# Attention followed by a mixture-of-experts layer: Q and K in fp16 parts, a new order of the softmax steps in the loop, and a new way to the scale factors in the lead-in

## The chip, the core and the metric

The kernel runs on one NeuronCore of one Trainium2 chip. The metric is device time in microseconds (us) of one launch. The engines are TensorE (PE in the profile, with PEld for its weight loads), VectorE (DVE), ScalarE (ACT), GpSimd (POOL) and SyncE (SP, which here only issues DMAs). Each has a queue of its own and works on it by itself; they meet through semaphores.

## The reference, cut to what matters

One sequence of S = 2048 rows and 256 columns goes through two residual blocks. The change touches the first:

```python
q = layernorm(x) @ dequant(wq) + bq          # 16 heads of 128; k and v likewise
scores = einsum('bqhd,bkhd->bhqk', q, k) / sqrt(128)
attn = softmax(scores, axis=-1)
out = einsum('bhqk,bkhd->bqhd', attn, v)     # 16 heads side by side: 2048 columns
y = out @ dequant(wo) + bo
x = x + layernorm(y)
```

`dequant(w)` is a matrix of 4-bit codes times a scale per 32 rows and column. The second block (`x + layernorm(ffn(layernorm(x)))`) routes each row to two of eight experts of width 176. Everything is float32 in the reference.

## The kernel before, in words

To keep accuracy with fast matmuls, each float32 operand is written as a high and a low part in a narrower type, and a product is made as three matmuls: high by high, high by low, low by high.

**Lead-in** (lines 221 to 374). The four chunks of x (512 rows each) are loaded, normalized (`ln0_stats`, `ln0_norm`), transposed by PE (`ln0_tr`) and split in fp16 parts `xnT` (`ln0_high` on ACT, `ln0_low` on DVE). The scales of the first pair of heads are spread over the partitions by a small matmul (`scale_bcast`), copied by ACT (`scale_s`) and multiplied with the codes on POOL (`dequant`). A power of two `sig`, taken from the largest scale of V, is found by an all-reduce over the partitions on POOL (line 341) and a few DVE steps; it keeps V's fp16 parts in range. Biases of Q and K are loaded by SP with one element per partition and head (lines 243 and 244).

**Projections.** `proj_qk` (line 179) makes 512 columns of K or Q for a head: four matmuls into one PSUM bank, ACT writes the high part with the bias (line 193, type fp32r), DVE the low part (line 194). `proj_v` (line 199) does the same for V in fp16 without a bias (lines 216 and 217). DVE's part is put into `pending` and issued by the next `flush()`.

**Attention loop** (lines 611 to 665). It runs over NS = 256 tiles g = 16 h + t: head h, and 128 query rows t. For a tile:

- `scores_half` twice: six matmuls per 1024 keys (lines 388, 389, 392; three PSUM buffers), then DVE's row maximum (line 393); `negmax` (line 399).
- `softmax`: ACT's exponentials of both halves, with row sums (line 406), into `p`.
- `recip`: DVE adds the two sums and inverts (lines 413 and 416).
- `high_part`: ACT writes p times the inverse as fp16 `ph` (line 420), SP transposes it by DMA into `pt`.
- `low_part`: the rest p/sum - ph as fp16 `pl`, 1536 columns on DVE (line 432), 512 on POOL (lines 438 and 439), and SP transposes that.
- `pv_part`: the product with V for a block of four tiles, 16 key chunks at three matmuls (lines 455 to 457); it is cut into eight `pv_unit`s per block, two units per pass, and runs PVLAG = 13 units behind. At the end of a block ACT and DVE write the output's parts (lines 463 and 464), and POOL issues their store.
- `fill`: one piece of projection for the next head or block (table `QK` for K and Q; V in between).

The order is written by hand (`manual_schedule`), so each engine's queue holds the instructions in the order of the code. One pass g of the loop before issues: s0(g) and its maximum; recip(g-1); pending parts; a PV unit; **high(g-1)**; s1(g) and its maximum; negmax(g); **exp(g)**; a PV unit; **low(g-1)**; fill(g).

**Tail.** It runs from line 943 on: the output projection reads the attention output back from DRAM (`load_oi`), then layernorm, router and experts. Its tiles `at` (line 681) and one `oi` tile (line 605) use the buffers of Q's tiles.

Of the kernel before, what the change touches and what calls it, by code (L numbers as in the profile page):

```python
# [20 lines left out]
S = 2048  # L21
# [16 lines left out]
def sandwich(  # L38
# [24 lines left out]
    # ---------------------------------------------------------------- constants  # L63
# [7 lines left out]
    bqT = const.tile([128, NH], F32)  # L71
    bkT = const.tile([128, NH], F32)
    sig = const.tile([128, 4], F32)
# [10 lines left out]
    ident_h = const.tile([128, 128], HP)  # L84
    iota8 = const.tile([128, 8], F32)
    one3 = const.tile([3, 128], F32)
    bvT = const.tile([128, NH], F32)
# [6 lines left out]
    def tail_consts(i):  # L94
        if i == 0:
            nc.sync.dma_start(out=bvT, in_=bv.rearrange("(h p) -> p h", p=128))
# [4 lines left out]
            nc.gpsimd.memset(one3, 1.0)  # L101
        else:
            nc.gpsimd.tensor_copy(ident_h, ident)
# [37 lines left out]

    def scale_s(which):
        f = sig[:, 1:2] if which == "v" else 1.0 / XS
        ps, sc, cd = raw[(0, which)]
        nc.scalar.activation(sc, ps, AF.Copy, scale=f)
        raw[(0, which)] = (sc, cd)

    def dequant(p, which):
        sc, cd = raw.pop((p, which))
        f = sig[:, 1:2] if which == "v" else 1.0 / XS  # L150
# [11 lines left out]
    # ------------------------------------------- LN of x, transposed in H and L  # L162
    # ------------------------------------------------------------- projections
# [15 lines left out]
    def proj_qk(which, h, b, tag="pj"):  # L179
        w = W[(h // 2, which)]  # L180
        bias = (bqT if which == "q" else bkT)[:, h : h + 1]
        ps = proj_psum(tag)
        col = bass.ts(h % 2, 128)
        n = 0
        for kc in range(2):
            for hl in range(2):
                nc.tensor.matmul(  # L187
                    ps, w[:, kc, col], xnT[:, 4 * b : 4 * b + 4, hl * 2 + kc, :],
                    start=(n == 0), stop=(n == 3),
                )  # L190
                n += 1
        t = kqv.tile([128, 2, 512], F32R, name=which + "T", bufs=8 if which == "k" else 2)
        nc.scalar.activation(t[:, 0, :], ps, AF.Identity, bias=bias)
        pending.append(lambda: nc.vector.scalar_tensor_tensor(
            t[:, 1, :], ps, bias, t[:, 0, :].bitcast(F32), ALU.add, ALU.subtract
        ))
        (Q if which == "q" else K)[(h, b)] = t
# [23 lines left out]
    with tc.tile_pool(name="start", bufs=4) as st:  # L221
# [3 lines left out]
        smax = st.tile([128, 128], F32, bufs=1)  # L225
        sc8 = st.tile([8, 3, 256], F32, bufs=1)
        nc.scalar.dma_start(out=s8, in_=sel8)
        for c in range(4):
            nc.sync.dma_start(out=xts[c], in_=xv[:, c])
        cds = {}  # L230
        for i, (which, codes, scales) in enumerate(
# [8 lines left out]
        nc.scalar.dma_start(  # L240
            out=smax, in_=wv_scales.rearrange("b (c n) -> (b c) n", n=128)
        )
        nc.sync.dma_start(out=bkT, in_=bk.rearrange("(h p) -> p h", p=128))
        nc.sync.dma_start(out=bqT, in_=bq.rearrange("(h p) -> p h", p=128))

        make_identity(nc, ident)
        def scale_bcast(which):
            i, cd = cds[which]
            if which == "v":
                ps = psA.tile([128, 512], F32, name="scv", tag="pv")  # L250
            else:
                ps = psS.tile([128, 2, 512], F32, name="scb", tag="s", bufs=3)[:, 0]
# [7 lines left out]
        sm = st.tile([128, 4], F32, bufs=1)  # L260
# [57 lines left out]
        def ln0_low(c):  # L318
# [5 lines left out]
        scale_bcast("k")  # L324
        scale_bcast("q")
        ln0_stats(0)
        ln0_stats(1)
        scale_s("k")
        scale_s("q")
        ln0_norm(0, nc.vector)  # L330
        ln0_tr(0)
        ln0_nb(1)
        ln0_norm(1, nc.scalar)
        ln0_tr(1)
        scale_bcast("v")
        dequant(0, "k")
        nc.vector.tensor_reduce(sm[:, 0:1], smax, AX.X, ALU.max)
        ln0_stats(2)
        ln0_high(0)
        nc.vector.tensor_scalar(sm[:, 1:2], sm[:, 0:1], 1e-30, None, ALU.max)  # L340
        nc.gpsimd.partition_all_reduce(
            sm[:, 2:3], sm[:, 1:2], 128, bass_isa.ReduceOp.max
        )
        ln0_stats(3, lambda: ln0_nb(2))
        dequant(0, "q")
        nc.vector.tensor_scalar(
            sm.bitcast(I32)[:, 3:4], sm.bitcast(I32)[:, 2:3], 0x7F800000, None,
            ALU.bitwise_and,
        )
        ln0_norm(2, nc.scalar)  # L350
        nc.vector.tensor_scalar(sig[:, 2:3], sm[:, 3:4], 0.125, None, ALU.mult)
        ln0_low(0)
        ln0_high(1)
        ln0_tr(2)
        nc.vector.reciprocal(sig[:, 0:1], sig[:, 2:3])
        ln0_norm(3, nc.vector)
        nc.vector.tensor_scalar(sig[:, 1:2], sig[:, 0:1], 1.0 / XS, None, ALU.mult)
        ln0_low(1)
        ln0_high(2)
        scale_s("v")  # L360
        ln0_low(2)
        proj_qk("k", 0, 0)
        ln0_tr(3)
        flush()
# [9 lines left out]
        dequant(0, "v")  # L374
# [4 lines left out]
    # --------------------------------------------------------------- attention  # L379
# [18 lines left out]
    def negmax(m):  # L398
        nc.vector.tensor_scalar(  # L399
            m[:, 2:3], m[:, 0:1], m[:, 1:2], -ISQ, ALU.max, ALU.mult  # L400
        )

    def softmax(h, t, ss, m):
        p = soft.tile([128, S], F32, name="p")
        for half in range(2):
            nc.scalar.activation(  # L406
                p[:, bass.ts(half, 1024)], ss[half].rearrange("p a b -> p (a b)"),
                AF.Exp, bias=m[:, 2:3], scale=ISQ, accum_out=m[:, 3 + half : 4 + half],
# [19 lines left out]
    def low_part(h, t, m, p, ph):  # L428
        pieces = 2 if h == 0 and t < 6 else 1
        cv = S - pieces * POOL_COLS  # L430
        pl = soft.tile([128, S], HP, name="pl")
        nc.vector.scalar_tensor_tensor(  # L432
            pl[:, :cv], p[:, :cv], m[:, 6:7], ph[:, :cv], ALU.mult, ALU.subtract
        )
        for c in range(cv, S, POOL_COLS):
            cs = slice(c, c + POOL_COLS)
            pr = soft.tile([128, POOL_COLS], F32, name="pr", bufs=1)
            nc.gpsimd.tensor_scalar(pr, p[:, cs], m[:, 6:7], 1.0, ALU.mult, ALU.mult)  # L438
            nc.gpsimd.tensor_tensor(pl[:, cs], pr, ph[:, cs], ALU.subtract)  # L439
# [32 lines left out]
    def fill(h, t):  # L472
# [22 lines left out]
    # ------------------------------- what the tail needs, made during the last head  # L495
# [75 lines left out]
    # ------------------------------------------------------------- attention loop  # L571
    PVLAG = 13
# [8 lines left out]
    def late(t):  # L581
# [22 lines left out]
        if t == 15:  # L604
            load_oi(0, 1, 1, "qT")
# [5 lines left out]
    for g in range(NS + 2):  # L611
# [20 lines left out]
        if prev is not None:  # L632
            hl = high_part(*prev)
# [44 lines left out]
    def op_mm(b, half, js, tag="pj"):  # L678
        if js[0] == 0:
            if half == 0:  # L680
                AT[b] = kqv.tile([128, 4, D], F32, name="at", tag="qT", bufs=2)
# [14 lines left out]
        if js[-1] == 3:  # L696
# [3 lines left out]
                at[:, tt], ps, sig[:, 2:3],  # L700
# [245 lines left out]
    nc.scalar.activation(sig[:, 3:4], sig[:, 2:3], AF.Sigmoid)  # L946
# [159 lines left out]
```

## Time and profile before

| what | value |
|---|---|
| runs | 1885.74, 1888.68, 1892.19 us; median 1888.68 |
| profiled execution | span 1897.5 us from first to last instruction; no other time of it is recorded |
| instructions | 25913 |
| granted PE clock, mean | 0.994 |
| PE, DVE, ACT, POOL busy | 1832.9, 1640.9, 1328.2, 883.7 us |
| first score matmul | 36.2 us |
| row maxima (line 393), first and last | 38.0 and 1600.1 us |
| exponentials (line 406) | 512 of 1.11 us, each followed by 0.19 us for the row sum |
| high part (line 420) | 256 of 2.00 us |
| low part on DVE (line 432), 1536 columns | 250 of 2.27 us in the mean, the shortest 1.82 |
| low part on POOL (line 438, line 439) | 262 of 0.72 and 262 of 1.86 us |
| DMA queues | 81.9% of 16 engines' span on the hardware queue that carries most transfers |

Where a row of the profile names an operation, it shows the output and the inputs by the program's names (`ph<-p,m`), the shape and type of each, how often, and the mean duration. PE's matmuls are pipelined, so their durations overlap; how far apart their starts lie says more. An idle time "<-" names what ended it; "issue" there means that the profile shows nothing waited for. Durations of neighbouring rows on DVE and ACT overlap by about 0.1 us too.

### The profile page before, as it was taken

To read this page: it belongs to the slowest core of one execution; us is meant where nothing else is said; L and a number is where in the kernel's file an instruction comes from. 1 tells how busy PE (TensorE), PEld (TensorE's weight loads), DVE (VectorE), ACT (ScalarE), POOL (GpSimd) and SP (SyncE) were. 2 spreads that over 40 slices of the span, in tenths; PEclk is the share of its full clock that TensorE was granted. 3 is DMA by queue.
4 is the path that set the end of the run, shared out by engine and by line. 5 is a ranking of instruction groups with operands and counts; after the bars stand their busy time and mean duration, and the time that the engine had idled before them with its cause. 6 is when DMAs were issued, how large, how long until landed. Compare 5 with 4: busy or idle time off the path is not lost.

```text
span 1897.5 us, 25913 instructions
## 1 busy us (share of the span) xinstructions
PE 1832.9 (97%) x8886; PEld 1161.5 (61%) x8886; DVE 1640.9 (86%) x2293; ACT 1328.2 (70%) x1730; POOL 883.7 (47%) x732
## 2 busy tenths in 40 slices
PE   5899999999999999999999999999999999899998
PEld 3555556555565565655655556655556555588887
DVE  5999998999999999999999999999999987468566
ACT  4877788778787778787878788777878777123232
POOL 2853465445444554455445544554444565233222
PEclk8999999999999999999999999999999999999999
DMA  2999999999999998899989988999899999982121
GB/s 75 192 188 179 179 207 184 188 184 194 192 184 182 208 202 186 183 193 204 183 174 199 205 180 187 190 210 185 181 186 192 222 222 243 257 250 70 51 68 56
DMA packets 1147220, 342.20 MB, mean 180 GB/s; under 512 B 1077008, under 2 KB 1137328, under 8 KB 1147088
## 3 DMA queue, kind: packets, MB, share of 16 engines
q1 hardware_dynamic: 1139152, 321.57, 81.9%
q0 software_dynamic: 5216, 16.81, 3.7%
q10 hardware_dynamic: 2720, 2.17, 0.4%
q8 instruction: 70, 1.15, 0.3%
q14 instruction: 62, 0.51, 0.1%
HBM read 53.08 MB, written 18.94 MB: 38 GB/s over the span
## 4 chain that ended last, share of the span: by engine, by line
PE 48%; DVE 9%; ACT 4%; DMA 4%; issue 3%; SPq 1%; POOL 0%; ACTq 0%; DVEq 0%; POOLq 0%
PE s L389 6%; PE s L388 6%; PE s L392 6%; PE pv L455 6%; PE pv L456 6%; PE pv L457 6%; PE gup L845 5%; DVE pl L432 4%; DMA pt<-pl 3%; PE pj L187 3%; ACT ph L420 3%; DVE m L393 2%; PE dps L884 2%; PE pj L206 1%; PE op L690 1%
## 5 line engine op out<-in xcount | busy, mean ns | idle before, releaser
L420 ACT ACTIVATE ph<-p,m 128x2048 f16<-128x2048 f32 x256 | 512.6, 2003 | 240.3 <-issue 134.9
L393 DVE TENSOR_REDUCE m<-s 128x1 f32<-128x1024 f32 x512 | 623.2, 1217 | 60.9 <-PE s L392 58.1
L406 ACT ACTIVATE p<-s,m 128x1024 f32<-128x1024 f32 x512 | 565.3, 1110 | 80.6 <-DVE m L399 76.4
L432 DVE SCALAR_TENSOR_TENSOR pl<-p,m,ph 128x1536 f16<-128x1536 f32 (+1 forms) x256 | 575.8, 2249 | 47.1 <-ACT ph L420 21.1
L439 POOL TENSOR_TENSOR pl<-pr,ph 128x512 f16<-128x512 f32 x262 | 486.5, 1857 | 264.7 <-issue 142.2
L388 PE MATMUL s<-kT,qT 128*128 128x512 f32 x1024 | 485.1, 474 | 5.3 <-ACT p L406 5.3
L389 PE MATMUL s<-kT,qT 128*128 128x512 f32 x1024 | 403.8, 394 | 0.0
L455 PE MATMUL pv<-pt,v 128*128 128x512 f16 x1024 | 393.4, 384 | 2.2 <-DVE o L464 2.0
L456 PE MATMUL pv<-pt,v 128*128 128x512 f16 x1024 | 388.7, 380 | 2.9 <-DMA pt<-pl 1.7
L457 PE MATMUL pv<-pt,v 128*128 128x512 f16 x1024 | 388.6, 379 | 0.0
L438 POOL TENSOR_SCALAR pr<-p,m 128x512 f32<-128x512 f32 x262 | 187.3, 715 | 329.5 <-DVE m L416 307.1
L392 PE MATMUL s<-kT,qT 128*128 128x512 f32 x1024 | 317.2, 391 | 0.0
L388 PEld LDWEIGHTS s<-kT,qT 128*128 128x128 f32 x1024 | 193.3, 189 | 79.0 <-ACT p L406 10.1
L392 PEld LDWEIGHTS s<-kT,qT 128*128 128x128 f32 x1024 | 192.2, 188 | 45.1
L389 PEld LDWEIGHTS s<-kT,qT 128*128 128x128 f32 x1024 | 193.5, 189 | 33.3
L455 PEld LDWEIGHTS <-v 128*128 128x128 f16 x1024 | 99.4, 97 | 185.7 <-issue 116.5
L457 PEld LDWEIGHTS <-v 128*128 128x128 f16 x1024 | 100.3, 98 | 121.2 <-issue 1.5
L456 PEld LDWEIGHTS <-v 128*128 128x128 f16 x1024 | 101.2, 99 | 75.3 <-issue 4.7
L859 POOL TENSOR_TENSOR hh<-sg,hh 128x512 fp32r<-128x512 f32 x42 | 54.5, 1299 | 143.6 <-ACT hh L858 106.6
L467 POOL DMA_DIRECT2D ot_d<-o x63 | 37.2, 590 | 172.8 <-DVE o L464 172.7
L858 ACT CAST hh<-sg 128x512 fp32r<-128x512 f32 (+1 forms) x45 | 27.5, 611 | 116.0 <-DVE sg L870 115.9
L406 ACT ACTIVATION_READ_ACCUMULATOR p<-s,m 128x1 f32 x512 | 99.7, 195 | 0.0
(160 smaller groups left out, 1727.5 us busy)
## 6 DMA issues: line engine op xcount, KB each, us to landing
oi<-ot_d SPq DMA_DIRECT2D x32, 512.0 KB, 5.9
ot_d<-o POOLq DMA_DIRECT2D x63, 256.0 KB, 5.4
pt<-ph SPq DMA_TRANSPOSE x256, 4.1
pt<-pl SPq DMA_TRANSPOSE x256, 4.0
cu<-ct_d SPq DMA_DIRECT2D x16, 256.0 KB, 3.7
xt<-in_L_attn_x SPq DMA_DIRECT2D x4, 512.0 KB, 5.2
wos<-in_L_attn_wo_scales ACTq DMA_DIRECT2D x32, 64.0 KB, 4.2
woc<-in_L_attn_wo_codes SPq DMA_DIRECT2D x8, 256.0 KB, 3.4
```

Source lines behind the costliest of these rows:

```text
L388: nc.tensor.matmul(s[:, j, :], q[:, 0, qc], k[:, 0, :], start=True, stop=False)
L389: nc.tensor.matmul(s[:, j, :], q[:, 0, qc], k[:, 1, :], start=False, stop=False)
L392: nc.tensor.matmul(s[:, j, :], q[:, 1, qc], k[:, 0, :], start=False, stop=True)
L393: nc.vector.tensor_reduce(m[:, half : half + 1], s.rearrange("p a b -> p (a b)"), AX.X, ALU.max)
L406: nc.scalar.activation(p[:, bass.ts(half, 1024)], ss[half].rearrange("p a b -> p (a b)"), AF.Exp, bias=m[:, 2:3], scale=ISQ, accum_out=m[: ...
L420: nc.scalar.activation(ph, p, AF.Copy, scale=m[:, 6:7])
L432: nc.vector.scalar_tensor_tensor(pl[:, :cv], p[:, :cv], m[:, 6:7], ph[:, :cv], ALU.mult, ALU.subtract)
L438: nc.gpsimd.tensor_scalar(pr, p[:, cs], m[:, 6:7], 1.0, ALU.mult, ALU.mult)
L439: nc.gpsimd.tensor_tensor(pl[:, cs], pr, ph[:, cs], ALU.subtract)
L455: nc.tensor.matmul(ps, vh, d[:, :, c, :], start=(c == 0), stop=False)
L456: nc.tensor.matmul(ps, vh, d[:, :, 16 + c, :], start=False, stop=False)
L457: nc.tensor.matmul(ps, vl, d[:, :, c, :], start=False, stop=(c == 15))
```

## The change

It does five things.

1. Q and K tiles become fp16 (`HP`) in place of fp32r. Their weights and biases are divided by powers of two `sig[:, 0]`, one each for Q, K and V, and the scale of the exponential and of `negmax` becomes a tensor `ssc`. In the loop (`wide=soft`) ACT writes the float32 projection to a scratch tile `t32`, and POOL makes both parts from it; in the lead-in ACT and DVE make them as before.
2. `low_part` is one DVE instruction over all 2048 columns; POOL's share and its scratch go. The addition of the two row sums goes from DVE to POOL (`row_sum`).
3. The order of a pass of the loop: s0(g); pending parts; PV unit; s1(g); negmax(g); exp(g); PV unit; **fill(g); recip(g-1); high(g-1); low(g-1); row_sum(g)**. `PVLAG` is 15, the loop has one more pass; `p` has three buffers, `ph` two.
4. The lead-in finds the three powers of two with PE: a maximum over scales and biases per partition on DVE, a transpose, a maximum and a bit mask on three partitions, and a matmul with a row of ones that spreads them. The scales of K and Q, not only V's, now wait for it. The biases come in as 48 rows and are transposed by PE.
5. In the tail `at` and one `oi` tile move to other buffers.

```diff
@@ proj_qk
-        t = kqv.tile([128, 2, 512], F32R, name=which + "T", bufs=8 if which == "k" else 2)
-        nc.scalar.activation(t[:, 0, :], ps, AF.Identity, bias=bias)
-        pending.append(lambda: nc.vector.scalar_tensor_tensor(
-            t[:, 1, :], ps, bias, t[:, 0, :].bitcast(F32), ALU.add, ALU.subtract
-        ))
+        t = kqv.tile([128, 2, 512], HP, name=which + "T", bufs=8 if which == "k" else 2)
+        if wide is None:
+            nc.scalar.activation(t[:, 0, :], ps, AF.Identity, bias=bias)
+            pending.append(lambda: nc.vector.scalar_tensor_tensor(
+                t[:, 1, :], ps, bias, t[:, 0, :], ALU.add, ALU.subtract
+            ))
+        else:
+            t32 = wide.tile([128, 512], F32, name="t32", bufs=1)
+            nc.scalar.activation(t32, ps, AF.Identity, bias=bias)
+            nc.gpsimd.tensor_copy(t[:, 0, :], t32)
+            nc.gpsimd.tensor_tensor(t[:, 1, :], t32, t[:, 0, :], ALU.subtract)
...
+        for i, scales in enumerate((wq_scales, wk_scales, wv_scales)):
+            nc.scalar.dma_start(
+                out=smax[:, i], in_=scales.rearrange("b (c n) -> (b c) n", n=128)
+            )
+        for i, bias in enumerate((bq, bk, bv)):
+            nc.scalar.dma_start(
+                out=b48[16 * i : 16 * i + 16], in_=bias.rearrange("(h p) -> h p", p=128)
+            )
...
-        nc.scalar.dma_start(
-            out=smax, in_=wv_scales.rearrange("b (c n) -> (b c) n", n=128)
-        )
-        nc.sync.dma_start(out=bkT, in_=bk.rearrange("(h p) -> p h", p=128))
-        nc.sync.dma_start(out=bqT, in_=bq.rearrange("(h p) -> p h", p=128))
...
+        def sig_bias():
+            ps = psA.tile([128, 512], F32, name="bps", tag="pj")
+            nc.tensor.transpose(ps[:, :48], b48, ident[:48, :48])
+            sgp["b"] = ps
+
+        def sig_local():
+            ps = sgp["b"][:, :48].rearrange("p (i h) -> p i h", i=3)
+            nc.vector.tensor_reduce(
+                sm[:, 3:5], ps[:, 0:2], AX.X, ALU.max, apply_absolute_value=True
+            )
+            nc.vector.scalar_tensor_tensor(
+                sm[:, 0:2], sm[:, 3:5], 1.0 / XS, sm[:, 0:2], ALU.mult, ALU.max
+            )
+            nc.vector.tensor_copy(bT, ps)
+
+        def sig_rows():
+            ps = psA.tile([128, 512], F32, name="smt", tag="pj")
+            nc.tensor.transpose(ps[:3, :128], sm[:, 0:3], ident)
+            sgp["t"] = ps
+
+        def sig_pow():
+            nc.vector.tensor_reduce(t3[:, 0:1], sgp["t"][:3, :128], AX.X, ALU.max)
+            nc.vector.tensor_scalar(t3[:, 1:2], t3[:, 0:1], 1e-30, None, ALU.max)
+            nc.vector.tensor_scalar(
+                t3.bitcast(I32)[:, 2:3], t3.bitcast(I32)[:, 1:2], 0x7F800000, None,
+                ALU.bitwise_and,
+            )
+            nc.vector.tensor_scalar(t3[:, 3:6], ident[:3, :3], t3[:, 2:3], None, ALU.mult)
+            ps = psA.tile([128, 512], F32, name="sgb", tag="pj")
+            nc.tensor.matmul(ps[:, :3], one3, t3[:, 3:6], start=True, stop=True)
+            sgp["s"] = ps
...
-        nc.gpsimd.partition_all_reduce(
-            sm[:, 2:3], sm[:, 1:2], 128, bass_isa.ReduceOp.max
-        )
...
@@ softmax steps
-            m[:, 2:3], m[:, 0:1], m[:, 1:2], -ISQ, ALU.max, ALU.mult
+            m[:, 2:3], m[:, 0:1], m[:, 1:2], ssc[:, 1:2], ALU.max, ALU.mult
...
-        p = soft.tile([128, S], F32, name="p")
+        p = soft.tile([128, S], F32, name="p", bufs=3)
...
-                AF.Exp, bias=m[:, 2:3], scale=ISQ, accum_out=m[:, 3 + half : 4 + half],
+                AF.Exp, bias=m[:, 2:3], scale=ssc[:, 0:1], accum_out=m[:, 3 + half : 4 + half],
...
+    def row_sum(m):
+        nc.gpsimd.tensor_scalar(
+            m[:, 5:6], m[:, 3:4], m[:, 4:5], 1.0 / PS, ALU.add, ALU.mult
+        )
+
     def recip(m):
-        nc.vector.tensor_scalar(
-            m[:, 5:6], m[:, 3:4], m[:, 4:5], 1.0 / PS, ALU.add, ALU.mult
-        )
         nc.vector.reciprocal(m[:, 6:7], m[:, 5:6])
...
-        ph = soft.tile([128, S], HP, name="ph", bufs=3)
+        ph = soft.tile([128, S], HP, name="ph")
...
-        pieces = 2 if h == 0 and t < 6 else 1
-        cv = S - pieces * POOL_COLS
         pl = soft.tile([128, S], HP, name="pl")
-        nc.vector.scalar_tensor_tensor(
-            pl[:, :cv], p[:, :cv], m[:, 6:7], ph[:, :cv], ALU.mult, ALU.subtract
-        )
-        for c in range(cv, S, POOL_COLS):
-            cs = slice(c, c + POOL_COLS)
-            pr = soft.tile([128, POOL_COLS], F32, name="pr", bufs=1)
-            nc.gpsimd.tensor_scalar(pr, p[:, cs], m[:, 6:7], 1.0, ALU.mult, ALU.mult)
-            nc.gpsimd.tensor_tensor(pl[:, cs], pr, ph[:, cs], ALU.subtract)
+        nc.vector.scalar_tensor_tensor(pl, p, m[:, 6:7], ph, ALU.mult, ALU.subtract)
...
-                proj_qk(kind, h + dh, b)
+                proj_qk(kind, h + dh, b, wide=soft)
@@ loop
-    PVLAG = 13
+    PVLAG = 15
...
-        if t == 15:
-            load_oi(0, 1, 1, "qT")
...
-    for g in range(NS + 2):
+    for g in range(NS + 3):
...
         if g == NS:
+            load_oi(0, 1, 1)
             load_oi(0, 1, 2)
             load_oi(0, 1, 3)
-        if prev is not None:
-            recip(prev[2])
         flush()
         if defer:
             pv_unit(2 * g - 1)
             defer = False
         pv_unit(2 * g)
-        if prev is not None:
-            hl = high_part(*prev)
         if live:
             s1 = scores_half(h, t, 1, m)
             negmax(m)
...
         if not first:
             pv_unit(2 * g + 1)
+        if live:
+            fill(h, t)
         if prev is not None:
+            recip(prev[2])
+            hl = high_part(*prev)
             low_part(*prev, hl)
         if live:
-            fill(h, t)
+            row_sum(m)
...
-                AT[b] = kqv.tile([128, 4, D], F32, name="at", tag="qT", bufs=2)
+                AT[b] = uwp.tile([128, 4, D], F32, name="at", bufs=2)
```

More of the change, by code (lines that the diff above doesn't have):

```diff
@@ L70, in sandwich @@
     nc.gpsimd.memset(nhalf, -0.5)
-    bqT = const.tile([128, NH], F32)
-    bkT = const.tile([128, NH], F32)
-    sig = const.tile([128, 4], F32)
+    bT = const.tile([128, 3, NH], F32)
+    bqs = const.tile([128, 2, NH], F32)
+    sig = const.tile([128, 4, 3], F32)
+    ssc = const.tile([128, 2], F32)
+    sgv = const.tile([128, 1], F32)
     def rstd_of(mv, n, pool):
@@ L83, in sandwich @@
     ident = const.tile([128, 128], F32)
-    ident_h = const.tile([128, 128], HP)
     iota8 = const.tile([128, 8], F32)
     one3 = const.tile([3, 128], F32)
-    bvT = const.tile([128, NH], F32)
+    bvT = bT[:, 2]
     bv3 = const.tile([128, NH, 3], BF)
@@ L95, in tail_consts @@
         if i == 0:
-            nc.sync.dma_start(out=bvT, in_=bv.rearrange("(h p) -> p h", p=128))
             nc.sync.dma_start(out=crow, in_=bo.partition_broadcast(128))
@@ L100, in tail_consts @@
                            allow_small_or_imprecise_dtypes=True)
-            nc.gpsimd.memset(one3, 1.0)
         else:
-            nc.gpsimd.tensor_copy(ident_h, ident)
             nc.gpsimd.tensor_copy(bv3[:, :, 0], bvT)
@@ L140, in load_w @@
         raw[(p, which)] = (sc, cd)
+    IX = {"q": 0, "k": 1, "v": 2}
     def scale_s(which):
-        f = sig[:, 1:2] if which == "v" else 1.0 / XS
+        f = sig[:, 2, IX[which] : IX[which] + 1]
         ps, sc, cd = raw[(0, which)]
@@ L149, in dequant @@
         sc, cd = raw.pop((p, which))
-        f = sig[:, 1:2] if which == "v" else 1.0 / XS
+        f = sig[:, 2, IX[which] : IX[which] + 1]
         if p > 0:
@@ L177, in proj_psum, with proj_qk @@
         return psA.tile([128, 512], F32, name="pj", tag=tag)
-    def proj_qk(which, h, b, tag="pj"):
+    def proj_qk(which, h, b, tag="pj", wide=None):
         w = W[(h // 2, which)]
-        bias = (bqT if which == "q" else bkT)[:, h : h + 1]
+        bias = bqs[:, IX[which], h : h + 1]
         ps = proj_psum(tag)
@@ L224, in sandwich @@
         s8 = st.tile([8, 2, 128], F32, bufs=1)
-        smax = st.tile([128, 128], F32, bufs=1)
+        smax = st.tile([128, 3, 128], F32, bufs=1)
+        b48 = st.tile([48, 128], F32, bufs=1)
         sc8 = st.tile([8, 3, 256], F32, bufs=1)
@@ L239, in sandwich, with scale_bcast @@
             cds[which] = (i, cd)
-        nc.scalar.dma_start(
-            out=smax, in_=wv_scales.rearrange("b (c n) -> (b c) n", n=128)
-        )
-        nc.sync.dma_start(out=bkT, in_=bk.rearrange("(h p) -> p h", p=128))
-        nc.sync.dma_start(out=bqT, in_=bq.rearrange("(h p) -> p h", p=128))
+        nc.gpsimd.memset(one3, 1.0)
         make_identity(nc, ident)
-        def scale_bcast(which):
+        def scale_bcast(which, ps):
             i, cd = cds[which]
[L249 to L252, printed above, removed]
             for kc in range(2):
@@ L258, in scale_bcast, with sig_all, sig_rest @@
             raw[(0, which)] = (ps.rearrange("p (k n) -> p k n", k=2), sc, cd)
-        sm = st.tile([128, 4], F32, bufs=1)
+        sm = st.tile([128, 8], F32, bufs=1)
+        t3 = st.tile([3, 6], F32, bufs=1)
+        sgp = {}
+        def sig_bias():
[26 more added lines that the diff above has]
+            sgp["s"] = ps
+        def sig_all():
+            nc.vector.tensor_scalar(sig[:, 0], sgp["s"][:, :3], 0.125, None, ALU.mult)
+            nc.vector.reciprocal(sig[:, 1], sig[:, 0])
+            nc.vector.tensor_scalar(sig[:, 2], sig[:, 1], 1.0 / XS, None, ALU.mult)
+        def sig_rest():
+            for i in range(2):
+                nc.vector.tensor_scalar(
+                    bqs[:, i], bT[:, i], sig[:, 1, i : i + 1], None, ALU.mult
+                )
+            nc.vector.scalar_tensor_tensor(
+                ssc[:, 0:1], sig[:, 0, 0:1], ISQ, sig[:, 0, 1:2], ALU.mult, ALU.mult
+            )
+            nc.vector.tensor_scalar(ssc[:, 1:2], ssc[:, 0:1], -1.0, None, ALU.mult)
         mvs, rs, nbs, xns, xps = {}, {}, {}, {}, {}
@@ L322, in ln0_low @@
             )
-        scale_bcast("k")
-        scale_bcast("q")
+        kq_ps = psS.tile([128, 2, 512], F32, name="scb", tag="s", bufs=3)
+        scale_bcast("k", kq_ps[:, 0])
+        scale_bcast("q", kq_ps[:, 1])
+        sig_bias()
         ln0_stats(0)
         ln0_stats(1)
-        scale_s("k")
-        scale_s("q")
+        nc.vector.tensor_reduce(sm[:, 0:3], smax, AX.X, ALU.max)
+        sig_local()
+        sig_rows()
         ln0_norm(0, nc.vector)
@@ L332, in sandwich @@
         ln0_nb(1)
+        sig_pow()
         ln0_norm(1, nc.scalar)
         ln0_tr(1)
-        scale_bcast("v")
-        dequant(0, "k")
[L337 to L340, printed above, removed]
-        nc.gpsimd.partition_all_reduce(
-            sm[:, 2:3], sm[:, 1:2], 128, bass_isa.ReduceOp.max
-        )
+        scale_bcast("v", psA.tile([128, 512], F32, name="scv", tag="pv"))
+        ln0_stats(2)
+        sig_all()
+        ln0_high(0)
+        scale_s("k")
+        dequant(0, "k")
+        ln0_low(0)
+        sig_rest()
         ln0_stats(3, lambda: ln0_nb(2))
+        ln0_high(1)
+        scale_s("q")
         dequant(0, "q")
-        nc.vector.tensor_scalar(
-            sm.bitcast(I32)[:, 3:4], sm.bitcast(I32)[:, 2:3], 0x7F800000, None,
-            ALU.bitwise_and,
-        )
         ln0_norm(2, nc.scalar)
-        nc.vector.tensor_scalar(sig[:, 2:3], sm[:, 3:4], 0.125, None, ALU.mult)
-        ln0_low(0)
-        ln0_high(1)
+        ln0_low(1)
         ln0_tr(2)
-        nc.vector.reciprocal(sig[:, 0:1], sig[:, 2:3])
         ln0_norm(3, nc.vector)
-        nc.vector.tensor_scalar(sig[:, 1:2], sig[:, 0:1], 1.0 / XS, None, ALU.mult)
-        ln0_low(1)
         ln0_high(2)
+        proj_qk("k", 0, 0)
+        flush()
+        ln0_low(2)
         scale_s("v")
-        ln0_low(2)
-        proj_qk("k", 0, 0)
         ln0_tr(3)
-        flush()
         ln0_high(3)
-        ln0_low(3)
+        dequant(0, "v")
         proj_qk("q", 0, 0, "pv")
         flush()
+        ln0_low(3)
         proj_qk("k", 0, 1, "s")
@@ L373, in sandwich @@
         flush()
-        dequant(0, "v")
     pt = pt_ctx.enter_context(tc.tile_pool(name="pt", bufs=2, reuse_waits="tile"))
@@ L407, in softmax, with recip @@
                 p[:, bass.ts(half, 1024)], ss[half].rearrange("p a b -> p (a b)"),
-                AF.Exp, bias=m[:, 2:3], scale=ISQ, accum_out=m[:, 3 + half : 4 + half],
+                AF.Exp, bias=m[:, 2:3], scale=ssc[:, 0:1], accum_out=m[:, 3 + half : 4 + half],
             )
         return p
-    def recip(m):
-        nc.vector.tensor_scalar(
+    def row_sum(m):
+        nc.gpsimd.tensor_scalar(
             m[:, 5:6], m[:, 3:4], m[:, 4:5], 1.0 / PS, ALU.add, ALU.mult
         )
+    def recip(m):
         nc.vector.reciprocal(m[:, 6:7], m[:, 5:6])
     def high_part(h, t, m, p):
-        ph = soft.tile([128, S], HP, name="ph", bufs=3)
+        ph = soft.tile([128, S], HP, name="ph")
         nc.scalar.activation(ph, p, AF.Copy, scale=m[:, 6:7])
@@ L563, in load_oi @@
         oi = kqv.tile(
-            [128, 4, 2, 256], HP, name="oi", tag=tag, bufs={"kT": 8, "v": 7, "qT": 2}[tag]
+            [128, 4, 2, 256], HP, name="oi", tag=tag, bufs={"kT": 8, "v": 7}[tag]
         )
@@ L665, in sandwich @@
             nc.sync.dma_start(out=X1[0], in_=XV[:, 0])
-    UEND = 2 * (NS + 2)
+    UEND = 2 * (NS + 3)
     AT, MV, XT, CT = {}, {}, {}, {}
@@ L699, in op_mm @@
             nc.vector.scalar_tensor_tensor(
-                at[:, tt], ps, sig[:, 2:3],
+                at[:, tt], ps, sig[:, 0, 2:3],
                 crow.unsqueeze(1).to_broadcast([128, 2, D]), ALU.mult, ALU.add,
@@ L945, in sandwich @@
     soft_ctx.close()
-    nc.scalar.activation(sig[:, 3:4], sig[:, 2:3], AF.Sigmoid)
+    nc.scalar.activation(sgv, ssc[:, 0:1], AF.Sigmoid)
     uwp = ctx.enter_context(tc.tile_pool(name="uw", bufs=1, side="right", reuse_waits="tile"))
```

## The prediction

> **What bounds the kernel now.** I read four views in this order: the page's engine totals, busy time by stretch, the waits of VectorE (DVE) and ScalarE (ACT), and the timeline of some tiles in the middle. "Tile" means one pass of the attention loop (one head, 128 query rows); there are 256.
>
> ```profile
> PE 1832.9 (97%) x8886; PEld 1161.5 (61%) x8886; DVE 1640.9 (86%) x2293; ACT 1328.2 (70%) x1730; POOL 883.7 (47%) x732
> ```
> ```profile
> 800.00:1200.00 400.00, 396.31 (x1833) 237.04 (x1833) 371.98 (x473) 317.96 (x406) 191.70 (x159) 1.00 0.92 191
> ```
> ```profile
> DVE m L393 <- PE s L392: 58.1, 139, 1.8
> ...
> DVE pl L432 <- ACT ph L420: 21.1, 69, 1.7
> ```
>
> In the stretch (columns PE, PEld, DVE, ACT, POOL) PE is busy 99%, DVE 93%, ACT 79%. The reductions L393 wait for PE's scores, and the chain of waits through this stretch is almost all PE. So PE bounds the loop, with DVE close behind. L393 starts at 37.99 us for the first tile and at 1597.91 for the last: 1559.9/255 = 6.117 us per tile.
>
> The timeline shows how DVE and ACT hand work to each other (columns: start, duration, engine, line, what; in brackets the idle time and who ended it):
>
> ```profile
> 889.11 0.21 DVE L399 TENSOR_SCALAR m<-m 128x1 f32<-128x1 f32 x1
> 889.24 1.95 DVE L432 SCALAR_TENSOR_TENSOR pl<-p,m,ph 128x1536 f16<-128x1536 f32 x1
> 889.42 1.12 ACT L406 ACTIVATE p<-s,m 128x1024 f32<-128x1024 f32 x1 [0.31 <-DVE m L399]
> 890.53 1.11 ACT L406 ACTIVATE p<-s,m 128x1024 f32<-128x1024 f32 x1
> 891.62 0.69 ACT L193 ACTIVATE kT<-pj,bkT 128x512 fp32r<-128x512 f32 x1
> ...
> 899.24 2.00 ACT L420 ACTIVATE ph<-p,m 128x2048 f16<-128x2048 f32 x1 [1.25 <-issue]
> 901.33 2.83 DVE L432 SCALAR_TENSOR_TENSOR pl<-p,m,ph 128x1536 f16<-128x1536 f32 x1 [0.19 <-ACT ph L420]
> ...
> 907.79 1.82 DVE L432 SCALAR_TENSOR_TENSOR pl<-p,m,ph 128x1536 f16<-128x1536 f32 x1
> 907.84 2.79 POOL L439 TENSOR_TENSOR pl<-pr,ph 128x512 f16<-128x512 f32 x1 [1.33 <-issue]
> 909.53 1.21 DVE L393 TENSOR_REDUCE m<-s 128x1 f32<-128x1024 f32 x1
> ```
>
> Two things are to be seen. First, on each engine the rows stand in the order in which the program issues them. Second, the order is a good one: ACT makes the high part of the tile before (L420) while DVE still reduces this tile's scores, so at L399 it is (nearly) ready. From there DVE makes the low part while ACT makes this tile's exponentials: the two run side by side.
>
> **The new order of the loop: the step that decides.** After the change a pass g issues on ACT: exp(g) twice, the projection's copy, then high(g-1). On DVE: reduce s0(g), pending low parts of V and o, reduce s1(g), negmax(g), the reciprocal, low(g-1). low(g-1) needs high(g-1), which now stands behind exp(g), which needs negmax(g). And negmax(g+1) stands behind low(g-1) in DVE's queue. So DVE waits through all of ACT's part of a tile, then ACT through all of DVE's. Queued behind the waiting low(g-1) are both reductions of the next tile; exp(g+1) waits for them. The third buffer of p and the later PVLAG don't break this ring: it is made by queue order, not by buffers. Its steps, from start to start in the rows:
>
> - negmax to exp: 0.33 (889.11 to 889.42; 0.33 at most tiles).
> - exp to exp 1.10, exp to the next ACT row 1.10 (889.42, 890.53, 891.62).
> - ACT's projection copies: 122 in the loop at 0.58, 98 V copies at 0.27 and 15 at 0.48 (rows of 0.68, 0.37, 0.58, of which 0.10 overlaps the next): 104.5/256 = 0.41.
> - high to low 2.09 (899.24 to 901.33).
> - low to the next reduction: 1.74 for 1536 elements beside nobody (907.79 to 909.53). The new one has 2048. The 1024-wide and 1536-wide rows have minima of 1.28 and 1.82, so 512 more cost 0.54: 2.28.
> - s0's reduction to the next row 1.13 (885.50 to 886.63).
> - DVE's low parts of V and o, 98 at 0.32, 15 at 0.59, 63 at 0.60: 78/256 = 0.30.
> - s1's reduction to negmax 1.25.
>
> Sum 10.0 us per tile against 6.117: 256 × 3.88 = +994 us.
>
> **The other parts, one by one.**
>
> *Q and K in fp16.* Score matmuls start 0.23 apart, the fp16 ones of PV 0.215 (899.70, 899.91, 900.13, 900.35, 900.56). Twelve per tile save 12 × 0.015 = 0.18 us of PE, 46 us in all, if PE were still the bound. In a ring of 10.0 PE has some 5.9 us of work and the saving is hidden: 0 taken. If the ring weren't there, this is what would show.
>
> *The split on GpSimd* takes 0.73 us (L194) off DVE in half the tiles; in the ring sum L194 is already left out. POOL loses L438 and L439 (0.69 and 1.16 undisturbed) in each tile and gets a copy and a subtraction in half of them. Nobody needs new K or Q for several tiles. But POOL can disturb DVE. Both 2.83 for DVE's low part at 901.33 and 2.79 for POOL at 907.84 are the undisturbed 1.82 and 1.17 plus a wait for the other. The Trainium skill ("SBUF — State Buffer", Who interferes with whom) calls it a lock held for a whole instruction, between a DVE instruction with two SBUF inputs and a GpSimd one that reads SBUF. By that rule a subtraction that starts just before low(g-1) adds up to 1.0 us in 127 tiles, +127 us; by the rows' timing it starts 0.68 + 0.1 + 0.69 = 1.47 after ACT's copy starts and ends at 1.47 + 1.16 = 2.63, while low(g-1) starts at 0.58 + 2.09 = 2.67. I take 0, as POOL falls under high(g-1), and keep +127 as the end of the range. A gain against 1.74 is excluded: that row was beside nobody.
>
> *Row sum on GpSimd*: 0.20 (L413) leaves DVE. It stands behind POOL's split, ready about 6 us after negmax(g-1), and is asked for at negmax(g), 10 us after it: 0. Cover gone, at most some 1 us.
>
> *ph in two buffers, PVLAG 15, and the SP queue.* The first transposes of a block wait on SP until the PV of the block two before has ended, unit 22 where it was 20. PE reaches it about 2 us after the next negmax; the row buffers are asked for again some 10 us later: 0, up to +20 if transposes pile up.
>
> *Lead-in.* Removed: the all-reduce on POOL. Around it POOL idles by "issue" 6.86 and 7.06 us and PE from 23.2 to 29.9. Two issues of biases on SP (0.64 and 5.18) go. Added: six issues on ACT's queue at 0.37 to 0.61, hidden before ACT's first work at 8.46, some 14 small DVE rows at 0.15 to 0.3, and two PE hops, on which K's and Q's weights now wait too. I take -6, ends -10 and +2. The first score matmul was at 36.2.
>
> *Tail.* Before, the last low part ended 12.6 us after the last negmax, with waits for the transposes of 3.1 and 3.4. By the ring it ends at 7.4 + 0.3 + 2.1 + 2.3 = 12.1. Two more PV units (12 × 0.215 = 2.6 us) fall into PE's gap at 1617 to 1620.7, and the oi load that moves to the loop's end joins two others on SP. 0, ends -4 and +6.
>
> *PE's clock.* In the ring PE idles some 4.2 us in each 10. The Trainium skill ("TensorE: Matmul & The Clock Gate", Why this matters for your kernels) warns of gaps over about 3 us: the clock falls to half. The trace agrees that it falls:
>
> ```profile
> 20.00:30.00 10.00, 1.54 (x4) 0.38 (x4) 3.13 (x7) 0.00 (x0) 2.53 (x3) 0.50 0.00 0
> ...
> 1612.00:1620.00 8.00, 4.76 (x42) 3.77 (x40) 4.32 (x7) 0.00 (x0) 0.97 (x2) 1.00 1.21 248
> 1620.00:1632.00 12.00, 11.31 (x70) 7.49 (x71) 3.10 (x10) 0.78 (x1) 1.04 (x1) 0.86 1.09 305
> ```
>
> After the 3.7 us gap before 1620.7 the clock reads 0.86 over 12 us, so it had come back within them. By the rule held all the time, PE would need 2 × 5.83 = 11.7 us per tile and become the bound; by these rows it recovers once PE is busy, and the slack of 4.2 us takes the loss. I take 0 and a granted clock of 0.8 to 1.
>
> **Sum.** 994 - 6 + 0 = +988. The profiled execution has a span of 1897.5, and nothing else of it is given; that is 8.8 over the runs' median of 1888.7. 1897.5 + 988 = 2885.5; less the same 8.8, 2877 us.
>
> **Rivals.**
> - *The ring with its price at the upper end* (POOL's lock, T = 10.5): 2877 + 127 = 3004. For it: DVE's median low part now is 2.39 instead of 1.82. Against: POOL has less to do and does it under high(g-1).
> - *The clock stays at half*: T = 11.7, 2877 + 256 × 1.66 = 3302. Against: a busy PE gets it back. 3%.
> - *Not slower: the low part really falls one tile later, and PE stays the bound.* That holds if low(g-1) doesn't hold up the next reductions, so that DVE finds high(g-1) done. DVE would then need 2.4 + 2.3 + 0.3 + 0.3 = 5.3 us, PE 5.94; -46 - 6 gives 1837. It decides from the point at which the ring is shorter than 5.94 us. Against: every row that I read is in program order, and in the new order low(g-1) directly follows on high(g-1), with exp(g) ahead of both. 6%.
>
> **How the numbers follow.** The ring as summed 75%, with the lock's price or a part of it 14%, the clock 3%, PE-bound 6%, a mixture near no change 2%. Range: the small terms at their low ends with a ring 0.2 shorter (2877 - 51 - 8) and the lock's price whole (3004): 2815 to 3005. About 0.3% is what a measurement of this kernel can tell from no change.
>
> **What would show it.** DVE's waits: low part for ph, about 4.6 us in each tile, some 1180 us in total (21.1 now). ACT's waits for negmax, about 5 us per tile (76.4 in total now). PE busy about 60% in the middle of the loop. Matmuls of the scores 0.215 apart. A reduction to the one two further on 10.0 us. No idle POOL around 20 to 27 us. I am wrong if DVE starts a reduction of the next tile before low(g-1), or if the loop has the PE waiting for nobody.

## The result and the profile after

The changed kernel takes 2933.2 us (median of 4 runs, 2932.3 to 2933.6) against 1890.2 (1885.7 to 1892.2): 1.5515 times as long, with a 95% interval of 1.5491 to 1.5538. The forecast was 2877, the range 2815 to 3005. In the profiled executions the span grew by 2931.6 - 1897.5 = 1034.1 us.

| stretch of the profiled execution | before | after | difference |
|---|---|---|---|
| start to the first row maximum | 38.0 | 31.8 | -6.2 |
| first to last row maximum | 1562.1 | 2601.2 | +1039.1 |
| last row maximum to the end | 297.4 | 298.7 | +1.3 |

The loss lies in the attention loop. The first line of its page, and the stretch 800 to 1200 us (PE, PEld, DVE, ACT, POOL busy, granted clock, DMA share, GB/s):

```profile
PE 2134.0 (73%) x8890; PEld 1002.9 (34%) x8890; DVE 1544.7 (53%) x1923; ACT 1347.6 (46%) x1730; POOL 738.3 (25%) x708
```
```profile
800.00:1200.00 400.00, 286.22 (x1103) 117.56 (x1102) 206.32 (x226) 192.05 (x243) 95.64 (x93) 0.84 0.61 113
```

No engine is full any more: in this stretch DVE is busy 52% and ACT 48%, which together make 100%. That is what two engines that take turns would look like. The waits name each other (us in total, times, longest):

```profile
ACT p L459 <- DVE m L471: 1331.6, 254, 5.8
DVE pl L485 <- ACT ph L475: 1251.4, 256, 6.6
```

L471 is the reciprocal. It stands right behind negmax (L452), whose result the exponential reads; the profile names the later of the two. Before, these were 76.4 (from negmax) and 21.1. One pass in the timeline, from one low part to the next:

```profile
1398.98 2.45 DVE L485 SCALAR_TENSOR_TENSOR pl<-p,m,ph 128x2048 f16<-128x2048 f32 x1 [4.72 <-ACT ph L475]
1401.35 1.21 DVE L446 TENSOR_REDUCE m<-s 128x1 f32<-128x1024 f32 x1
1402.48 0.41 DVE L223 TENSOR_TENSOR v<-pj,v 128x256 f16<-128x256 f32 x1
1402.82 1.21 DVE L446 TENSOR_REDUCE m<-s 128x1 f32<-128x1024 f32 x1
1404.06 0.27 DVE L452 TENSOR_SCALAR m<-m,ssc 128x1 f32<-128x1 f32 x1
...
1404.45 1.21 ACT L459 ACTIVATE p<-s,m,ssc 128x1024 f32<-128x1024 f32 x1 [5.50 <-DVE m L471]
...
1405.65 1.20 ACT L459 ACTIVATE p<-s,m,ssc 128x1024 f32<-128x1024 f32 x1
...
1406.83 0.68 ACT L200 ACTIVATE t<-pj,bqs 128x512 f32<-128x512 f32 x1
1407.40 2.00 ACT L475 ACTIVATE ph<-p,m 128x2048 f16<-128x2048 f32 x1
1407.57 0.61 POOL L201 CAST kT<-t 128x512 f16<-128x512 f32 x1 [8.29 <-ACT t L200]
1408.26 1.16 POOL L202 TENSOR_TENSOR kT<-t,kT 128x512 f16<-128x512 f32 x1
...
1409.43 2.35 DVE L485 SCALAR_TENSOR_TENSOR pl<-p,m,ph 128x2048 f16<-128x2048 f32 x1 [5.03 <-ACT ph L475]
1409.51 2.41 POOL L466 TENSOR_SCALAR m<-m 128x1 f32<-128x1 f32 x1
```

No two of the DVE and ACT rows of the ring run at the same time, apart from the 0.1 us by which neighbours overlap: DVE from 1398.98 to 1404.4, ACT from 1404.45 to 1409.4, then DVE again. The pass took 10.45 us. Over all passes, a row maximum follows its counterpart in the tile before after 10.19 us (6.117 before).

### The profile page after: what moved, and what is told of

Read it like the earlier page. It is cut to its first block, busy times and chain, and to the rows that moved or that the text cites. A ratio compares the mean times of both kernels' runs of the same rounds, so it can differ in the third digit from the quotient of the medians.

```text
span 2931.6 us, 25133 instructions
## 1 busy us (share of the span) xinstructions
PE 2134.0 (73%) x8890; PEld 1002.9 (34%) x8890; DVE 1544.7 (53%) x1923; ACT 1347.6 (46%) x1730; POOL 738.3 (25%) x708
## 4 chain that ended last, share of the span: by engine, by line
DVE 42%; ACT 33%; issue 14%; PE 9%; DMA 1%; ACTq 1%; POOL 0%; SPq 0%; POOLq 0%; DVEq 0%
DVE m L446 20%; ACT ph L475 16%; DVE pl L485 16%; ACT p L459 13%; PE gup L890 3%; ACT t L200 2%; DVE v L223 1%; DVE m L471 1%; DVE o L510 1%; PE dps L929 1%; ACT v L222 1%; PE op L735 1%; PE op_s L735 1%; PE pv L501 1%; PE pv L503 1%
## 5 line engine op out<-in xcount | busy, mean ns | idle before, releaser
L485 DVE SCALAR_TENSOR_TENSOR pl<-p,m,ph 128x2048 f16<-128x2048 f32 x256 | 603.2, 2356 | 1251.4 <-ACT ph L475 1251.4
L459 ACT ACTIVATE p<-s,m,ssc 128x1024 f32<-128x1024 f32 x512 | 612.2, 1199 | 1335.6 <-DVE m L471 1331.6
L501 PE MATMUL pv<-pt,v 128*128 128x512 f16 x1024 | 445.5, 435 | 274.5 <-DVE o L510 224.5
L441 PE MATMUL s<-kT,qT 128*128 128x512 f16 x1024 | 451.2, 441 | 239.0 <-ACT p L459 239.0
L466 POOL TENSOR_SCALAR m<-m 128x1 f32<-128x1 f32 x256 | 327.6, 1280 | 560.7 <-ACT p L459 549.0
L442 PE MATMUL s<-kT,qT 128*128 128x512 f16 x1024 | 451.5, 441 | 0.0
L502 PE MATMUL pv<-pt,v 128*128 128x512 f16 x1024 | 442.0, 432 | 0.0
L503 PE MATMUL pv<-pt,v 128*128 128x512 f16 x1024 | 437.9, 428 | 0.0
L445 PE MATMUL s<-kT,qT 128*128 128x512 f16 x1024 | 357.2, 435 | 0.0
L442 PEld LDWEIGHTS <-qT 128*128 128x128 f16 x1024 | 111.4, 109 | 402.1 <-issue 322.5
L201 POOL CAST qT<-t 128x512 f16<-128x512 f32 x63 | 38.5, 611 | 662.6 <-ACT t L200 662.6
L187 PE MATMUL pj<-xnT,wk 128*128 128x512 f16 x252 | 84.6, 470 | 133.2 <-DVE v L223 132.4
L445 PEld LDWEIGHTS <-qT 128*128 128x128 f16 x1024 | 112.4, 110 | 159.4 <-issue 67.4
L441 PEld LDWEIGHTS <-qT 128*128 128x128 f16 x1024 | 111.7, 109 | 151.0 <-issue 62.5
L187 PE MATMUL pj<-xnT,wq 128*128 128x512 f16 x256 | 77.7, 433 | 101.6 <-DVE v L223 101.6
L459 ACT ACTIVATION_READ_ACCUMULATOR p<-s,m,ssc 128x1 f32 x512 | 99.0, 193 | 0.0
```

Source lines behind the costliest of these rows:

```text
L187: nc.tensor.matmul(ps, w[:, kc, col], xnT[:, 4 * b : 4 * b + 4, hl * 2 + kc, :], start=(n == 0), stop=(n == 3),)
L441: nc.tensor.matmul(s[:, j, :], q[:, 0, qc], k[:, 0, :], start=True, stop=False)
L442: nc.tensor.matmul(s[:, j, :], q[:, 0, qc], k[:, 1, :], start=False, stop=False)
L445: nc.tensor.matmul(s[:, j, :], q[:, 1, qc], k[:, 0, :], start=False, stop=True)
L459: nc.scalar.activation(p[:, bass.ts(half, 1024)], ss[half].rearrange("p a b -> p (a b)"), AF.Exp, bias=m[:, 2:3], scale=ssc[:, 0:1], accum ...
L466: nc.gpsimd.tensor_scalar(m[:, 5:6], m[:, 3:4], m[:, 4:5], 1.0 / PS, ALU.add, ALU.mult)
```

## The experiments

Ten kernels made eleven runs. All ratios are to the kernel before, run beside them on the same chip, whose median lay between 1895 and 1901 us there. The runs are spread over three chips; where two of them are compared, the ratios say more than the times.

### The order alone, put into the kernel before

```diff
-        if prev is not None:
-            recip(prev[2])
         flush()
...
-        if prev is not None:
-            hl = high_part(*prev)
...
-        if prev is not None:
-            low_part(*prev, hl)
         if live:
             fill(h, t)
+        if prev is not None:
+            recip(prev[2])
+            hl = high_part(*prev)
+            low_part(*prev, hl)
```

> The kernel before with the new order of a pass alone (projection, recip, high part and low part behind the exponentials; nothing else of the change). Theory: the same ring, with 0.33 + 1.10 + 1.10 + 0.41 + 2.09 + (1.74 alone or 2.75 behind GpSimd's share) + 1.13 + 0.30 + 0.32 + 1.25 = 9.8 to 10.8 us per tile, 2830 to 3085 us. Rival (the loss needs the new arithmetic): near 1890.

Measured: 2905.4 us, ratio 1.529 (1.5226 to 1.5355), 10.11 us per tile. With fp32r scores, GpSimd's share of the low part and the old lead-in all in place, the order by itself makes nearly the whole loss. The waits are those of the changed kernel:

```profile
ACT p L406 <- DVE m L413: 1361.4, 253, 6.2
DVE pl L432 <- ACT ph L420: 1140.6, 255, 5.1
```

### The change with the old order

```diff
+        if prev is not None:
+            recip(prev[2])
         flush()
...
         pv_unit(2 * g)
+        if prev is not None:
+            hl = high_part(*prev)
...
-        if live:
-            fill(h, t)
         if prev is not None:
-            recip(prev[2])
-            hl = high_part(*prev)
             low_part(*prev, hl)
         if live:
             row_sum(m)
+            fill(h, t)
```

(with PVLAG 13, two buffers of p, three of ph)

> All of the change stays, but the loop gets its old order back: recip and high part of the tile before ahead of this tile's second scores, low part behind the exponentials, projection last; PVLAG 13, two buffers of p and three of ph as before; the row sum on GpSimd stands ahead of the projection. Theory (the ring of exponentials, high part, low part and reductions makes the whole loss): PE bounds the loop again with fp16 scores, 5.95 us per tile, 1837 us, up to 1860 if GpSimd's row sum comes late. Rival (the arithmetic of the change costs something by itself, such as the longer exponentials or the 2048-wide low part): clearly over 1890, and if the order were not the cause at all, near 2930.

Measured: 1894.6 us, ratio 0.9971 (0.9944 to 0.9998). So the loss also needs the order: with the old one (and the old lag and buffers, which the run with the order alone had as well) nothing of it is left. But the 1837 to 1860 of the theory didn't come, and 1894.6 lies just over the 1890 that the rival named: something other than the order still costs what the fp16 scores save, and holds the loop at 6.13 us per tile in the mean. The repeat with more rounds:

> The kernel e1 once more with more rounds, beside the two others on one chip. Theory: 0.3% under the kernel before, which its interval should now separate from no change. Rival: the same as before within the interval.

Measured: 1896.2 us, ratio 0.9982 (0.9967 to 0.9996).

### The low part one pass later

The changed kernel; only the place of the low part moves.

```diff
         if prev is not None:
             recip(prev[2])
-            hl = high_part(*prev)
-            low_part(*prev, hl)
+        if held is not None:
+            low_part(*held)
+            held = None
+        if prev is not None:
+            held = (*prev, high_part(*prev))
```

> The changed kernel with one thing moved: the low part of a tile is issued one pass later, behind the next tile's maxima and ahead of that tile's high part; buffers and PVLAG stay. Theory: DVE then finds the high part done and no longer waits for ACT within a pass; the ring opens and the loop goes at PE's pace, 6.0 us per tile, 1840 to 1880 us in all. Rival (DVE and ACT are bound by something else than the position of the low part, for instance ACT's high part standing behind the exponentials): at least 9 us per tile, over 2600 us.

Measured: 1945.8 us, ratio 1.024 (1.0211 to 1.0269), 6.29 us per tile. The rival is out by far: the wait of the low part for a high part of the same pass is what closes the ring. The theory's 1840 to 1880 is missed as well. ACT still waits 316.9 us for DVE, and in 62 passes DVE waits 127.3 us for ACT's part of o, which in the timeline stands behind a high part.

### More matmuls

```diff
+            for _ in range(2):
+                nc.tensor.matmul(s[:, j, :], q[:, 0, qc], k[:, 0, :], start=True, stop=True)
             nc.tensor.matmul(s[:, j, :], q[:, 0, qc], k[:, 0, :], start=True, stop=False)
```

> The changed kernel with eight more score matmuls per tile (the first one of each group is made three times, the last overwrites). That is 8 x 0.215 = 1.7 us more of PE per tile, 440 us in all. Theory: PE has over 3 us of slack per tile in the ring and its clock is not on the path: the time stays within 0.5% of 2933, and the granted clock in the loop rises above 0.85 as PE's gaps shrink. Rival (PE, slowed by its clock, is part of the path): +100 to +440 us.

Measured: 2942.8 us, ratio 1.549 (1.5448 to 1.5532), where the changed kernel has 1.5515 (1.5491 to 1.5538). Eight more matmuls per tile are hidden, and the clock in the same stretch went from 0.84 to 0.94:

```profile
800.00:1200.00 400.00, 323.48 (x1414) 141.40 (x1412) 204.97 (x224) 191.76 (x242) 97.23 (x94) 0.94 0.63 116
```

More matmuls at a higher clock, and a time 0.3% longer: neither PE's work nor its clock is on the path.

### The scale as a constant

```diff
-                AF.Exp, bias=m[:, 2:3], scale=ssc[:, 0:1], accum_out=m[:, 3 + half : 4 + half],
+                AF.Exp, bias=m[:, 2:3], scale=ISQ, accum_out=m[:, 3 + half : 4 + half],
```

(and -ISQ for `ssc[:, 1:2]` in `negmax`)

> The changed kernel with the scale of the exponentials and of negmax as a constant in the instruction again instead of the tensor ssc, so that the scale is left out of the result. Theory (each exponential takes 1.20 us instead of 1.11 because its scale is read from a tensor, and negmax 0.27 instead of 0.21; three such rows lie in the ring): 0.25 us less per tile, 64 us, so 2870. Rival (the longer exponentials have another cause, such as the PSUM accesses of the fp16 scores): within 10 us of 2933.

Measured: 2872.8 us, 60.4 under the changed kernel, 9.97 us per tile instead of 10.19. The two rows, changed kernel first (count, busy us, mean ns, idle before):

```profile
L459 ACT ACTIVATE p<-s,m,ssc 128x1024 f32<-128x1024 f32 x512 | 612.2, 1199 | 1335.6 <-DVE m L471 1331.6
```
```profile
L459 ACT ACTIVATE p<-s,m 128x1024 f32<-128x1024 f32 x512 | 565.5, 1109 | 1318.2 <-DVE m L471 1309.0 <-PE pj L187 5.3 <-DVE m L452 3.9
```

0.09 us per exponential comes from where the scale is read. The Trainium skill ("ScalarE: Activation LUTs", What ACT_TABLE_LOAD costs) has that price: about 93 ns for each operand of one value per partition. The rows agree, 1199 against 1109 ns.

### What holds the version with the old order

The DMA engines' share was the suspect: 1.07 of a long stretch with the old order, 0.94 in the kernel before, 0.61 in the changed one, with the same transposes in each. So the transposes of the low part were left out, and PV reads the high part in their place:

```diff
-        nc.sync.dma_start_transpose(
-            out=PT[(h, t // 4)][:, t % 4, 16:32, :], in_=pl
-        )
...
-            nc.tensor.matmul(ps, vh, d[:, :, 16 + c, :], start=False, stop=False)
+            nc.tensor.matmul(ps, vh, d[:, :, c, :], start=False, stop=False)
```

> The kernel e1 (change with the old order) without the DMA transposes of the low part of the probabilities; the PV matmuls that read it read the high part instead, so that part of the result is left out and PE's work stays the same. Theory (in e1 the DMA transposes bound the loop: DMA share 1.06 of the stretch, about 6.1 us of all 16 DMA engines per tile, which ate the saving of the fp16 scores): the loop falls to PE's 5.95 us, 256 x 0.18 = 46 us under e1, about 1848 us. Rival (a wait between DVE, ACT and PE bounds e1): within 10 us of e1's 1894.6.

Measured: 1824.9 us, ratio 0.9613 (0.9587 to 0.9639), 5.87 us per tile. The long stretch (400 to 1400 us) of the version with the old order, and of the same without those transposes:

```profile
400.00:1400.00 1000.00, 962.92 (x4572) 446.32 (x4571) 864.13 (x933) 819.77 (x1017) 261.25 (x398) 0.99 1.07 190
```
```profile
400.00:1400.00 1000.00, 992.88 (x4762) 463.58 (x4761) 904.84 (x973) 854.63 (x1057) 253.68 (x412) 1.00 0.59 110
```

The DMA share falls to 0.59, and PE fills up to 99%: only then is it the bound, and the saving of the fp16 scores shows. The loop gains 63 us on the kernel before (5.87 against 6.117 us per tile), more than the 46 counted for the score matmuls; the rest isn't explained.

It is not a steady limit, though. With the old order the median tile takes 5.83 us, as it does without those transposes; the mean of 6.13 comes from about a quarter of the tiles, which are longer. Over 5.83 there are 76 us in all, and 41 of them fall into 21 tiles: the third, sixth and ninth of the seven heads in which the next pair's weights are loaded, each right behind a load (42 of 78 in the repeat; without the low part's transposes these 21 tiles have no excess at all). The longest, 11.51 us, begins at 821.24:

```profile
816.22 1.92 SPq L130 DMA_DIRECT2D st_s<-in_L_attn_wv_scales  x4
818.18 0.43 SPq L135 DMA_DIRECT2D st_c<-in_L_attn_wv_codes  x1
818.71 3.49 SPq L478 DMA_TRANSPOSE pt<-ph  x1
...
827.87 0.59 PE L502 MATMUL pv<-pt,v 128*128 128x512 f16 x1 [3.07 <-DMA pt<-pl]
...
827.92 2.56 DVE L485 SCALAR_TENSOR_TENSOR pl<-p,m,ph 128x2048 f16<-128x2048 f32 x1 [3.36 <-DMA pt<-pl]
```
```profile
817.00:820.00 3.00, 3.00 (x16) 1.35 (x14) 2.43 (x3) 2.47 (x2) 1.09 (x1) 1.00 0.28 79
```

SP issues the loads ahead of the next transposes, the DMA share drops to 0.28, and the transposes come late: PE and DVE wait for them. That the loads are the cause is argued from these rows; no run moved them. Nor is it settled whether the DMA engines are short or SP's queue. The engines move 190 GB/s here and 191 in the kernel before, at shares of 1.07 and 0.94; SP spends 878 of the 1000 us of the stretch issuing transposes, 708 in the kernel before and 390 without those of the low part. Leaving them out relieves both.

> The kernel before with the same omission (no transposes of the low part, PV reads the high part in its place; that part of the result is left out). Theory (before, PE bounds the loop with fp32r scores, and the transposes lie just under it): within 0.7% of 1890. Rival (the transposes bound the kernel before too): 1860 or less.

Measured: 1919.1 us, ratio 1.011 (1.0086 to 1.0134). Both lines missed: with less for the DMA engines to do, the kernel before got slower. Its low part on DVE has now a median of 2.56 us instead of 2.39:

```profile
L432 DVE SCALAR_TENSOR_TENSOR pl<-p,m,ph x256: 1278/2556/2832, 49.2 to 1633.9; 128x1536 f16<-128x1536 f32 x125, 128x1024 f16<-128x1024 f32 x3
```

The undisturbed 1.82 is met less often (32 rows take 1.8 to 1.95 us, 111 in the kernel before), so DVE and GpSimd collided in more tiles; DVE is busy 945 of 1000 us in the long stretch, 929 before. That the shift in time brings the collisions is argued, not shown: no kernel took GpSimd's share alone away from the kernel before. What is shown is that fewer transposes alone don't make the kernel before faster.

### fp32r scores, the split, and the row sum in the old order

Three variants of the version with the old order. First, Q and K as fp32r, parts made by ACT and DVE:

> The kernel e1 with Q and K as fp32r again, ACT writing the high part and DVE the low part as before (the tail's at tile goes back to Q's buffers). Theory (PE and DMA transposes are nearly level, so the narrower scores bring almost nothing): 0 to 15 us over e1, 1895 to 1910. Rival (the saving of 0.18 us per tile was real in e1 and something else in the change costs as much): 40 us or more over e1, from 1935.

Measured: 1917.4 us, ratio 1.0105 (1.0078 to 1.0132). 23 us over: between the two lines. Second, fp16, but parts made by ACT and DVE:

> The kernel e1 with fp16 Q and K split by ACT and DVE also in the loop, not by GpSimd. It stands between e1 (1894.6) and e1r (fp32r, split by ACT and DVE, 1917.4). Theory (e1r lost by PE's slower fp32r matmuls, DVE has 0.5 us of room per tile): within 8 us of e1. Rival (e1r lost by the 0.65 us that the split costs DVE in half the tiles): 1910 to 1920.

Measured: 1891.0 us, ratio 0.9954 (0.994 to 0.9967). As the theory had it; the 26 us between these two (1.5% by the ratios) are the price of fp32r here, somewhat over half of the 46 that PE's matmuls alone would make. GpSimd as the place of the split gains nothing. This is the fastest complete version of the study. Third, the row sum on DVE:

> The kernel e1 with the addition of the two row sums on DVE again, ahead of the reciprocal, as before. Theory (the transposes bound e1, DVE has room for 0.2 us per tile): within 6 us of e1. Rival (GpSimd's row sum, which waits for DVE's lock[...], comes late and costs e1 time): 10 us or more under e1, 1885 or less, which would make it the fastest complete version.

Measured: 1917.4 us, ratio 1.0095 (1.0082 to 1.0108): 21 us slower than the repeat on the same chip (1896.2), against both lines. GpSimd's row sum isn't late in this order; it takes a row off the way from the exponentials to the high part. From the second exponential to its tile's high part it is 2.81 us with the sum on DVE, 2.32 on GpSimd (medians over the tiles). Here the ordinary tiles get longer, 5.94 us in the median instead of 5.83, and not the few late ones. Why stays open.

## Why the prediction was right, step by step

**The ring** is shown: the order alone makes it in the kernel before, and undoing the order removes it. Its terms, as means over all passes from the starts in the trace:

| step | predicted | measured |
|---|---|---|
| negmax to exp | 0.33 | 0.39 |
| exp to exp | 1.10 | 1.20 |
| second exp, projection copy, to the high part | 1.10 + 0.41 | 1.62 |
| high part to low part | 2.09 | 2.04 |
| low part to the next reduction | 2.28 | 2.28 |
| first to second reduction | 1.13 + 0.30 | 1.44 |
| reduction to negmax | 1.25 | 1.25 |
| sum | 10.0 | 10.2 |

**The mis-sized term.** The two exponentials and the negmax were taken over from the old rows although their scale had become a tensor; that part of the change was given no price at all, though the page named above had one. The run with constants took 60 us off and brought the period to 9.97, the 10.0 of the forecast. In it the first three lines are 0.33, 1.10 and 1.55, so the scale made 0.06 + 0.09 + 0.07 = 0.22 us of each tile; the 0.04 left in the third line is made up by the high part, 0.05 under its forecast.

Of the 56 us between 2877 and 2933, 45 lie in the loop (1039.1 for 994) and 1 in the ends. The other 10 come from the last step of the sum. It took off the 8.8 us by which the span of the profiled execution of the kernel before lay over the runs' median, as if the new kernel's would lie as far over; but that one has a span of 2931.6 and a time of 2933.4, at the median of its runs.

**GpSimd's lock at nothing.** Right: the new low part has a minimum of 2.350 and a median of 2.351, so the split at 1407.57 and 1408.26 falls under the high part. It was close: the margin was 0.04 us in the forecast, and 0.007 in the trace (median of the 122 passes with a split). The low part follows its high part after the same 0.03 us with a split and without. The other side of the lock shows at 1409.51: GpSimd's row sum on a single column takes about 2.4 beside the low part, in 122 of the 256 tiles, and 0.26 where it comes before.

**PE's clock** fell to 0.84 in the loop, inside 0.8 to 1, and cost nothing, as the run with more matmuls shows.

**Lead-in and tail.** -6.2 where -6 was taken, +1.3 where 0 was. The version with the old order has its first maximum at 31.3 as well, so the gain of the lead-in is independent of the loop.

**The waits foretold**: 1251 for "some 1180", 1332 for "about 5 per tile". PE's busy share is 72% for "about 60%": with the granted clock at 0.84 in that stretch a score matmul (L441) has a mean of 441 ns, 382 with the old order at 0.99.

**What was wrong in it: the rival on the other side.** It gave 1837 for a loop with its order intact, and saw PE as the bound with only DVE close behind. With the order intact the change gets 1895 and 1896. The stretch that it quoted has the DMA share in its last column but one, 0.92, and that wasn't counted as a bound: with a faster PE the share goes to 1.07 and some tiles wait for them, and without half of them the time goes to 1825.

## What to carry to other kernels

In a loop written out by hand, follow one pass around each pair of engines: if engine A waits within the pass for B, and B within the same pass for A, the period is the sum of both parts, with three buffers of p here as with two in the run with the order alone. Two engines whose busy shares add up to about 100% and which name each other in the waits are the picture of it. And before a saving on the bounding engine is counted, read the other columns of that stretch, the DMA share too, and put the median tile beside the mean: what takes the saving back may sit in a few tiles.

## What the runs showed that I had not expected

- An exponential of 128x1024 from PSUM takes 1.20 us with its scale in a tensor and 1.11 with a constant; a row of one column on DVE (negmax) 0.27 against 0.21.
- A GpSimd instruction on one column per partition took 2.41 us beside DVE's low part and 0.26 alone.
- With the old order most tiles go at PE's pace; over half of what is lost against it lies in 21 tiles of 256 behind weight loads.
- Taking away half of the transposes made the kernel before slower (1919 against 1895), and the same step made the version with fp16 scores faster (1825 against 1895).
